# The first layer of a graph network: the product of the two e columns moved from VectorE to TensorE, shift and clamp in one operation

## The chip, the cores and the metric

The kernel runs on one core of a Trainium2 chip. A core has a matrix engine (TensorE, PE in the profile), a vector engine (VectorE, DVE), an engine for activation functions (ScalarE, ACT), a general engine (GpSimd, POOL) and SyncE (SP), which here only issues DMAs. Each engine takes its instructions in program order; they meet through semaphores. Matmuls write to PSUM[...]; everything else lies in SBUF or in DRAM. The metric is the device time of one launch in microseconds, and less is better.

## The reference, cut to what matters

Four graph layers follow each other on 4096 nodes with 128 features, each added to its input and normalised. Only the first, a hyperbolic graph convolution, is touched. With h the nodes as points of the unit ball it computes

```python
x_tangent = logmap0(h)
x_local = jax.vmap(lambda xi: logmap(xi, h))(h)          # 4096 x 4096 x 128, never formed by the kernel
logits = (x_tangent @ wl)[:, None] + (x_tangent @ wr)[None, :] + att_b[0]
adj_att = adj * jax.nn.sigmoid(logits)
support_t = jnp.einsum('ij,ijd->id', adj_att, x_local)
```

logmap(xi, hj) is a multiple of the Moebius difference of the two points, so the sum over j needs, for each pair (i, j), one scalar factor that depends on the distance alone, and products with matrices of node features. The kernel scales the nodes to g, takes e = sqrt(1/4 + g.g) for each node, and finds the factor from

t(i, j) = e(i) e(j) - g(i).g(j), not less than 1/4 + 5e-7,

as log(4t + 2s) / s, where s is the square root of 4t*t - 1/4. The factor is symmetric in i and j, the sigmoid is not.

## The kernel before

The rows and columns of the 4096 x 4096 matrices are cut into eight blocks of 512. `pair_loop` goes over the 36 pairs of blocks (I, J) with I not above J; each of the 28 pairs of two different blocks serves both (I, J) and (J, I), the 8 diagonal ones serve one side. Each tile of a pair has 128 partitions and 4 x 512 elements. For one pair the steps of the work are:

- `load`: the 512 x 512 adjacency block of each side comes from DRAM by SP (1 MB each; two buffers). On a new row of pairs it also broadcasts the rows di and ei to all partitions, otherwise dj.
- `turn_adj`, four (or eight) times: PE transposes 512 x 128 of it into PSUM (ptA, two buffers). `copy` takes the result to the tile `at` on ScalarE, `vcopy` does the same on VectorE. `store` writes `at` to DRAM for the later layers.
- `distance`, four times: PE multiplies g by g into PSUM (pz, two buffers, which it shares with `turn`).
- `shift`, four times: VectorE forms t from the broadcast row ei, the column ex and pz, in one scalar_tensor_tensor: ei * ex - pz.
- `clamp`: VectorE takes the maximum of the whole tile and the lower limit into y.
- `square`, `ln`, `root`, `inverse`, `log` on ScalarE, `add_root` and `phi` on VectorE: the factor, in the tile t.
- `sigmoid` on ScalarE (four activations a side), `mask` on VectorE (times the adjacency), `first` on VectorE (times the factor).
- `turn` on PE (the factor transposed, four times) and `second` on VectorE (times it), for the other side of the pair.
- `sum_i`, `sum_j` on PE: the products with the features; `add_i`, `add_j` on VectorE: added up.

The order is written out by hand in `PAIR_ORDER` (line 32 on): a list of entries name.k.ahead. In step i each entry is issued for pair i + ahead, so work of up to five pairs stands side by side; the list sets the order in every engine's queue, and nothing reorders it later. Adjacency blocks with k of 4 or more, `turn`, `second`, `sum_j` and `add_j` are left out for a diagonal pair. ScalarE works with sets of tables: sigmoid is in one set, logarithm and exponential in another, and a change between them is an instruction of its own. `sigmoid` loads the second set after its last side (line 609).

Ahead of the loop `layer0` computes the columns. e lies in the second half of the tile `de` (line 395, ex at line 411) beside d, the column of the logits; PE turns `de`, ScalarE evacuates it (line 428) and SP stores it as `rows` in DRAM (line 429), from where the broadcasts take it.

Of the kernel before, what the change touches and what calls it, by code (L numbers as in the profile page):

```python
# [9 lines left out]
F32 = mybir.dt.float32  # L10
F32R = mybir.dt.float32r
AF = mybir.ActivationFunctionType
ALU = mybir.AluOpType
# [3 lines left out]
P = 128  # L17
# [7 lines left out]
S = 512  # L25
# [4 lines left out]


PAIR_ORDER = """
turn_adj.4.0 first.0.-1 copy.4.0 distance.2.1 second.3.-1 mask.0.0 ln.0.0 turn_adj.1.1 turn.1.-1
root.0.0 sum_i.1.-2 turn_adj.0.1 shift.2.1 copy.1.1 copy.0.1 mask.1.0 load.1.1 add_i.0.-2 add_root.0.0
store.1.0 sum_j.0.-2 distance.1.1 turn_adj.3.1 turn_adj.5.1 inverse.0.0 sum_i.0.-1 second.1.-1
add_j.0.-2 distance.0.1 log.0.0 shift.1.1 sigmoid.0.1 vcopy.3.1 distance.3.1 turn_adj.2.1 add_j.1.-2
vcopy.5.1 sum_i.3.-1 phi.0.0 shift.0.1 load.0.2 turn_adj.7.1 sum_i.2.-1 copy.2.1 turn.2.0 shift.3.1
clamp.0.1 turn.0.0 turn_adj.6.1 vcopy.7.1 sigmoid.1.1 second.2.0 copy.6.1 second.0.0 square.0.1
sum_j.1.-1 store.0.1 turn.3.0
"""  # L40


class Net:
# [226 lines left out]
    def layer0(self, x, weight, bias, att_w, att_b):  # L270
        nc, tc, N, NT, D = self.nc, self.tc, self.N, self.NT, self.D
# [3 lines left out]
        with ExitStack() as ctx:  # L275
# [4 lines left out]
            pre = pre_pools.enter_context(tc.tile_pool(name="pre0", bufs=2))  # L280
# [4 lines left out]
            HT = keep.tile([P, N], F32, tag="HT", name="HT")  # L285
            HA = keep.tile([P, NT, D + 1], F32, tag="HA", name="HA")
# [31 lines left out]
            p = self.ps_t.tile([P, 4, P], F32, tag="pt", name="pt")  # L318
# [14 lines left out]
            for g in self.groups():  # L333
                s = slice(g[0], g[-1] + 1)
                p = self.ps_t.tile([P, 4, P], F32, tag="pt", name="pt")
# [55 lines left out]
            b = self.ts("b", hsq, -1.0, ALU.mult, 1.0, ALU.add)  # L391
            nc.vector.tensor_scalar(b, b, MIN_NORM, None, op0=ALU.max)
            rb = self.rec("rb", b)
            ga, gb = self.tt("ga", ca, rb, ALU.mult), self.tt("gb", cb, rb, ALU.mult)
            de = self.cols.tile([P, 2, NT], F32, tag="de", name="de")
            gg = self.col("gg")
            for g in self.groups():
                p = self.ps_t.tile([P, 4, P], F32, tag="pt", name="pt")
# [9 lines left out]
                nc.gpsimd.tensor_tensor(squares[:, 0, :, :], H[:, s, :], H[:, s, :], ALU.mult)  # L408
                nc.vector.tensor_reduce(gg[:, s], squares[:, 0, :, :], AX.X, ALU.add)

            ex = de[:, 1, :]
            nc.vector.tensor_scalar(ex, gg, 0.25, None, op0=ALU.add)
            nc.scalar.activation(ex, ex, AF.Sqrt)
            nc.vector.tensor_scalar(rb, ex, 0.5, None, op0=ALU.add)
            nc.vector.reciprocal(b, rb)

            at = self.artanh_over("ah", hn)
            dl, dr = de[:, 0, :], self.col("dr")
# [2 lines left out]
                nc.vector.scalar_tensor_tensor(d, cb, hw[:, k : k + 1], d, op0=ALU.mult, op1=ALU.add)  # L421
                nc.vector.tensor_tensor(d, d, at, ALU.mult)
            nc.vector.tensor_scalar(dl, dl, attb, None, op0=ALU.add)
            rows = self.dram.tile([2, N], F32, tag="rows", name="rows")
            p = self.ps_t.tile([P, 4, P], F32, tag="pt", name="pt")
            nc.tensor.transpose(p[0 : 2 * NT, 0, :], de.rearrange("p k t -> p (k t)"), self.ident)
            e2 = pre.tile([2 * NT, P], F32, tag="e2", name="e2")
            nc.scalar.copy(e2, p[0 : 2 * NT, 0, :])
            nc.sync.dma_start(out=rows.rearrange("k (t p) -> (k t) p", p=P), in_=e2)
            b2x, bhalf = self.ts("b2x", b, 2.0, ALU.mult), self.ts("bhalf", b, 0.5, ALU.mult)  # L430

            hp1 = self.ts("hp1", b, -1.0, ALU.mult, 2.0, ALU.add)
# [2 lines left out]
            nc.vector.memset(self.quarter, -0.25)  # L435

            pre_pools.close()
            self.pair_loop(HT, HA, dr, ex, rows)


            x0 = HT.rearrange("p (t d) -> p t d", d=D)
# [70 lines left out]
                if t % 4 == 3:  # L512
                    self.normalise_tile(t // 4, on_scalar=True)

    def pair_loop(self, HT, HA, dr, ex, rows):

# [2 lines left out]
        nc, tc, NS, D = self.nc, self.tc, self.NS, self.D  # L521
        with ExitStack() as ctx:
# [3 lines left out]
            wk = ctx.enter_context(tc.tile_pool(name="wk0", bufs=2))  # L526
# [4 lines left out]
            pairs = [(I, J) for I in range(NS) for J in range(I, NS)]  # L531
            n = len(pairs)
            st = [{} for _ in pairs]
            row = {}

            def sides(p):

                I, J = pairs[p]
                return [(I, J)] if I == J else [(I, J), (J, I)]

            def broadcast(k, I, tag):

                t = wk.tile([P, S], F32, tag=tag, name=tag)
                nc.sync.dma_start(out=t, in_=rows[k, I * S : (I + 1) * S].partition_broadcast(P))
                return t

            def once(p, key, pool, tag, shape=(4, S), **kw):

                if key not in st[p]:
                    st[p][key] = pool.tile([P, *shape], F32, tag=tag, name=tag, **kw)  # L550
                return st[p][key]

            def load(p, k):
                I, J = pairs[p]
                if k == 0:
                    if I == J:
                        row["d", I] = broadcast(0, I, "di")
                        row["e", I] = broadcast(1, I, "ei")
                    else:
                        row["d", J] = broadcast(0, J, "dj")  # L560
                    st[p]["d"] = [row["d", i] for i, _ in sides(p)]
                    st[p]["e"] = row["e", I]
                i, j = sides(p)[k]
                nc.sync.dma_start(
                    out=once(p, f"ad{k}", adp, "ad"),
                    in_=self.adj[i * S : (i + 1) * S, j * S : (j + 1) * S].rearrange("(a p) c -> p a c", p=P),
                )

            def turn_adj(p, m):
                pt = ps_t.tile([P, 4, P], F32, tag="pt", name="ptA")  # L570
# [14 lines left out]
            def distance(p, b):  # L585
                I, J = pairs[p]
                pz = ps_z.tile([P, S], F32, tag="pz", name="pz")
                j = 4 * J + b
                nc.tensor.matmul(  # L589
                    pz, lhsT=HT[:, j * P : (j + 1) * P], rhs=HT[:, I * S : (I + 1) * S], start=True, stop=True  # L590
                )
                st[p]["pz", b] = pz

            def shift(p, b):
                j = 4 * pairs[p][1] + b
                nc.vector.scalar_tensor_tensor(  # L596
                    once(p, "t", wk, "t")[:, b, :], st[p]["e"], ex[:, j : j + 1], st[p].pop(("pz", b)),
                    op0=ALU.mult, op1=ALU.subtract,
                )

            def sigmoid(p, k):
                J = sides(p)[k][1]
                w = once(p, f"w{k}", wtp, "w")
                for jb in range(4):
                    nc.scalar.activation(  # L605
                        w[:, jb, :], st[p]["d"][k], AF.Sigmoid, bias=dr[:, 4 * J + jb : 4 * J + jb + 1]
                    )
                if k == len(sides(p)) - 1:
                    nc.scalar.preload_act_table_set("natural_log_exp_and_others")

            def mask(p, k):
                w = st[p][f"w{k}"]
                nc.vector.tensor_tensor(w, w, st[p][f"at{k}"], ALU.mult)  # L613

            def clamp(p, _):
                y = once(p, "y", wk, "y", bufs=1)
                nc.vector.tensor_scalar(y, st[p]["t"], 0.25 + 5e-7, None, op0=ALU.max)

            def square(p, _):
                nc.scalar.activation(st[p]["y"], st[p]["y"], AF.Square, scale=2.0)  # L620

            def ln(p, _):
                nc.scalar.activation(st[p]["y"], st[p]["y"], AF.Ln, bias=self.quarter)

            def root(p, _):
                nc.scalar.activation(once(p, "s", wk, "s", bufs=1), st[p]["y"], AF.Exp, scale=0.5)

            def inverse(p, _):
                nc.scalar.activation(st[p]["y"], st[p]["y"], AF.Exp, scale=-0.5)

            def add_root(p, _):
# [1 line left out]
                nc.vector.scalar_tensor_tensor(t, t, 2.0, st[p]["s"], op0=ALU.mult, op1=ALU.add)  # L633

            def log(p, _):
                t = st[p]["t"]
                nc.scalar.activation(t, t, AF.Ln, scale=2.0)

# [63 lines left out]
            def add_i(p, _):  # L702
# [7 lines left out]
            whole = {"load", "store", "sigmoid", "mask"}  # L710
            work = dict(
                load=load, turn_adj=turn_adj, copy=copy, vcopy=vcopy, store=store, distance=distance, shift=shift,
                sigmoid=sigmoid, mask=mask, clamp=clamp, square=square, ln=ln, root=root, inverse=inverse,
                add_root=add_root, log=log, phi=phi, first=first, turn=turn, second=second, sum_i=sum_i, sum_j=sum_j,
                add_j=add_j, add_i=add_i,
            )
            order = [(name, int(k), int(ahead)) for name, k, ahead in (o.split(".") for o in PAIR_ORDER.split())]

            def step(i):


                for name, k, ahead in order:
                    p = i + ahead
                    if not 0 <= p < n:
                        continue
                    two = len(sides(p)) == 2
                    if two or not (
                        name in pair_only or name in whole and k == 1 or name in blocks and k >= 4
                    ):
                        work[name](p, k)  # L730

            reach = [ahead for _, _, ahead in order]
# [814 lines left out]
```

## Time and profile before

| what | us |
|---|---|
| median of 3 runs (2209.81 to 2211.59) | 2210.46 |
| the profiled execution, of which the times below come | 2210.88 |
| its span, from the first to the last instruction | 2209.1 |
| ahead of the pair loop, 0 to 71 | 71 |
| the pair loop, 71 to 774 | 703 |
| the rest: the end of the first layer and the three other layers | 1435 |

In the stretch from 71 to 774 us TensorE is busy for 579.4 us, VectorE for 672.7, ScalarE for 678.9 and GpSimd for 26.7 (the last of it work for what follows the loop). The DMA engines have a mean share of 0.62.

The groups of the loop that the change touches, from the page of the whole execution:

| line and operation | count | mean ns |
|---|---|---|
| L596 VectorE, shift, 512 elements, one operand in PSUM | 144 | 740 |
| L617 VectorE, clamp, 2048 elements | 36 | 1231 |
| L577 ScalarE, adjacency copy from PSUM, 512 elements | 164 | 578 |
| L577 VectorE, the same copy | 92 | 683 |
| L589 PE, records of the distances (two to a matmul) | 288 | 628 |

How to read the views: a line of the page gives the source line, the engine, the operation, output and inputs with their sizes, the count, the busy time with the mean of one, and the idle time just before with what ended it. A line of the timeline gives start, length, engine, line, operation, tiles and the number of neighbours merged; in brackets stands how long the engine was idle before and what released it. A row of the windows view gives a stretch, its length, and how long each engine was busy in it with its number of instructions, then the clock of TensorE that was granted, the share of the DMA engines' time and what they moved.

### The profile page before, as it was taken

The numbers are of one execution on the slowest core, as the hardware profiler recorded it, in microseconds if no ns is written. First come the engines' busy times: TensorE is split into PE (matmuls) and PEld (weight loads), VectorE is DVE, ScalarE is ACT, GpSimd is POOL, SyncE is SP. The second block draws the span as 40 slices with busy tenths as digits, with TensorE's granted clock in tenths as the row PEclk, the third lists the DMA queues.
The fourth block names the chain that finished last, engine by engine and source line by source line (L and its number), as shares of the span: only waits on it lengthen the run. The fifth ranks groups of instructions, "written<-read, shape, count | busy, mean of one in ns | idle before, by whom it ended". The sixth has DMA issues, their size and how long they took to land.

```text
span 2209.1 us, 24056 instructions
## 1 busy us (share of the span) xinstructions
PE 1947.3 (88%) x8720; PEld 1048.7 (47%) x8720; DVE 1882.1 (85%) x2732; ACT 1476.3 (67%) x1858; POOL 105.7 (5%) x146
## 2 busy tenths in 40 slices
PE   4488888888888708999999999999998999989998
PEld 4266666666666605433333333333333444434443
DVE  6699999999999987789999999999897344558887
ACT  5699999999999974687777787877883222210000
POOL 2000000000000432210000000000000000000000
PEclk7689999999999956999999999999998999999999
DMA  2466566666666407884646465565456777767883
GB/s 55 143 210 234 205 243 209 229 200 228 213 208 212 156 0 246 210 229 172 198 163 190 172 198 181 174 191 175 169 194 232 281 269 272 254 234 270 290 300 111
DMA packets 112868, 448.44 MB, mean 203 GB/s; under 512 B 9760, under 2 KB 20064, under 8 KB 71776
## 3 DMA queue, kind: packets, MB, share of 16 engines
q1 hardware_dynamic: 94160, 361.82, 46.5%
q10 hardware_dynamic: 9360, 68.16, 9.1%
q0 software_dynamic: 9216, 16.78, 4.2%
q8 instruction: 73, 1.20, 0.2%
q14 instruction: 59, 0.48, 0.1%
HBM read 369.10 MB, written 77.63 MB: 202 GB/s over the span
## 4 chain that ended last, share of the span: by engine, by line
PE 41%; DVE 34%; ACT 17%; issue 5%; DMA 3%; ACTq 0%; POOL 0%; SPq 0%; DVEq 0%; POOLq 0%
PE pv L919 10%; PE pa L1253 10%; PE pa L1430 9%; DVE e L902 8%; PE ps L893 5%; DVE w L613 3%; ACT e L900 3%; ACT w L605 3%; DVE t L596 2%; DVE w L645 2%; DVE nat L883 2%; DVE t L641 2%; DVE w L656 2%; DVE t L633 1%; ACT at L577 1%
## 5 line engine op out<-in xcount | busy, mean ns | idle before, releaser
L902 DVE SCALAR_TENSOR_TENSOR e<-at,e 128x2048 f32<-128x2048 f32 x256 | 583.0, 2287 | 70.2 <-ACT e L900 69.5
L900 ACT ACTIVATE e<-ps 128x1024 f32<-128x1024 f32 x512 | 493.3, 1024 | 146.9 <-PE ps L893 126.1
L919 PE MATMUL pv<-e,VA 128*64 128x512 f32 x2048 | 497.0, 606 | 7.1 <-DVE e L902 6.3
L893 PE MATMUL ps<-QS,KS 128*128 128x512 f32 x1024 | 313.0, 425 | 4.3 <-issue 2.0
L893 PEld LDWEIGHTS ps<-QS,KS 128*128 128x128 f32 x1024 | 172.0, 189 | 230.0 <-ACT e L900 173.4
L919 PEld LDWEIGHTS pv<-e,VA 128*64 128x64 f32 x2048 | 124.9, 136 | 249.3 <-issue 214.8
L1253 PE MATMUL pa<-ring,Y 128*128 128x512 f32 x512 | 229.2, 602 | 0.0
L573 PE MATMUL ptA<-ident,ad 128*128 128x128 f32 x1024 | 158.5, 283 | 62.0 <-ACT at L577 50.0
L1430 PE MATMUL pa<-w,F 128*128 128x512 f32 x448 | 197.0, 598 | 0.0
L573 PEld LDWEIGHTS ptA<-ident,ad 128*128 128x128 f32 x1024 | 119.8, 144 | 142.0 <-ACT at L577 98.0
L1427 DVE SCALAR_TENSOR_TENSOR w<-rho,col,ring 128x512 f32<-128x512 f32 x224 | 162.8, 747 | 25.5 <-PE pa L1430 13.1
L589 PE MATMUL pz<-HT 128*128 128x512 f32 x288 | 151.3, 628 | 22.1 <-DVE w L656 16.5
L668 PE MATMUL pi<-HA,w 128*128 128x129 f32 x1152 | 154.4, 279 | 0.8 <-DVE w L645 0.8
L1253 PEld LDWEIGHTS pa<-ring,Y 128*128 128x128 f32 x512 | 97.4, 194 | 114.3 <-issue 113.8
L613 DVE TENSOR_TENSOR w<-w,at 128x2048 f32<-128x2048 f32 x64 | 146.1, 2283 | 0.5 <-ACT at L577 0.5
L668 PEld LDWEIGHTS pi<-HA,w 128*128 128x128 f32 x1152 | 142.2, 195 | 4.0 <-issue 2.3
L1430 PEld LDWEIGHTS pa<-w,F 128*128 128x128 f32 x448 | 84.3, 191 | 107.2 <-issue 79.5
L874 ACT ACTIVATE nat<-nat 128x2048 f32<-128x2048 f32 x64 | 122.6, 1916 | 3.5 <-DMA nat<-in_adj_dram 3.5
L596 DVE SCALAR_TENSOR_TENSOR t<-ei,de,pz 128x512 f32<-128x512 f32 x144 | 103.8, 740 | 16.0 <-PE pz L589 8.4
L683 PE MATMUL pj<-HA,w 128*128 128x129 f32 x896 | 109.5, 274 | 2.7 <-DVE w L656 2.7
L683 PEld LDWEIGHTS pj<-HA,w 128*128 128x128 f32 x896 | 104.6, 191 | 2.9 <-DVE w L656 2.9
L577 ACT COPY at<-ptA 128x512 f32<-128x512 f32 x164 | 91.2, 578 | 14.2 <-PE ptA L573 13.8
(359 smaller groups left out, 2443.8 us busy)
## 6 DMA issues: line engine op xcount, KB each, us to landing
ring<-adjT SPq DMA_DIRECT2D x128, 1024.0 KB, 5.1
ad<-in_adj_dram SPq DMA_DIRECT2D x64, 1024.0 KB, 5.3
adjT<-at SPq DMA_DIRECT2D x64, 1024.0 KB, 4.9
nat<-in_adj_dram ACTq DMA_DIRECT2D x64, 1024.0 KB, 5.0
at<-adjT SPq DMA_DIRECT2D x63, 1024.0 KB, 4.8
qk<-cut SPq DMA_DIRECT2D x16, 512.0 KB, 11.4
KS<-qk POOLq DMA_DIRECT2D x32, 256.0 KB, 7.6
QS<-qk POOLq DMA_DIRECT2D x32, 256.0 KB, 5.3
```

Source lines behind the costliest of these rows:

```text
L573: nc.tensor.transpose(pt[:, ib, :], ad[:, ib, jb * P : (jb + 1) * P], self.ident)
L589: nc.tensor.matmul(pz, lhsT=HT[:, j * P : (j + 1) * P], rhs=HT[:, I * S : (I + 1) * S], start=True, stop=True)
L613: nc.vector.tensor_tensor(w, w, st[p][f"at{k}"], ALU.mult)
L668: nc.tensor.matmul(row[I, "po"][ib // 2][:, ib % 2, :], lhsT=st[p]["w0"][:, jb, ib * P : (ib + 1) * P], rhs=HA[:, 4 * J + jb, :], start=False,
L683: nc.tensor.matmul(pj[:, a, :], lhsT=st[p]["w1"][:, ib, jb * P : (jb + 1) * P], rhs=HA[:, 4 * I + ib, :], start=(ib == 0), stop=(ib == 3),)
L893: nc.tensor.matmul(p[:, h, :], lhsT=KS[:, h2 + h, jb * P : (jb + 1) * P], rhs=QS[I % 2][:, h2 + h, :], start=True, stop=True,)
L900: nc.scalar.activation(e[:, h2 : h2 + 2, :], p, AF.Exp)
L902: nc.vector.scalar_tensor_tensor(e, at[:, jb % 4, :].unsqueeze(1).to_broadcast([P, NH, S]), 0.0, e, op0=ALU.not_equal, op1=ALU.mult,)
L919: nc.tensor.matmul(st["po"][h // 2][g : g + 64, :], lhsT=VA[:, o : o + 64], rhs=e[:, h, :], start=(jb == 0), stop=(jb == NT - 1), skip_gro ...
L1253: nc.tensor.matmul(st["pa"], lhsT=Y[:, 4 * J + jb, :], rhs=at[:, jb, :], start=False, stop=(J == NS - 1 and jb == 3), skip_group_check=True,)
L1427: nc.vector.scalar_tensor_tensor(w, rho[:, I * S : (I + 1) * S], col[:, 0, j : j + 1], at[:, jb, :], op0=ALU.max, op1=ALU.mult)
L1430: nc.tensor.matmul(pa, lhsT=F[:, j, :], rhs=w, start=False, stop=(j == NT - 1), skip_group_check=True)
```

## The change

The product e(i) e(j) is computed by PE and added to the distances in the PSUM tile, so that pz holds g.g - e.e. Each e is split into two parts, which the type float32r (one pass of PE) holds: the first rounded, the second what is left, rounded. The four products of parts are four contraction rows of one matmul: `er` holds the rows (part 1, part 2, part 1, part 2) for block I, `el` the negated rows (1, 1, 2, 2) for block J. `shift` is then one tensor_scalar from PSUM: times -1, maximum with the lower limit. `clamp` and ei are gone; `square` reads t and writes y.

What else changes: `layer0` makes the parts on VectorE, turns three columns instead of two, evacuates the turned tile twice (plain on ScalarE, negated on VectorE) and stores five rows with two DMAs. A function `vectors`, called at the head of every step for the pair farthest ahead, issues the di and dj broadcasts on SP and the loads of er and el on GpSimd (which converts to float32r). The change of tables is now placed in front of the first logarithm or exponential after a sigmoid. And `PAIR_ORDER` is another list: among other things the loads come later, `first` and `mask` of a pair's second side stand a step behind, four adjacency blocks of eight go to VectorE (0, 1, 2, 6) instead of three (3, 5, 7).

```diff
-turn_adj.4.0 first.0.-1 copy.4.0 distance.2.1 second.3.-1 mask.0.0 ln.0.0 turn_adj.1.1 turn.1.-1
-root.0.0 sum_i.1.-2 turn_adj.0.1 shift.2.1 copy.1.1 copy.0.1 mask.1.0 load.1.1 add_i.0.-2 add_root.0.0
-store.1.0 sum_j.0.-2 distance.1.1 turn_adj.3.1 turn_adj.5.1 inverse.0.0 sum_i.0.-1 second.1.-1
-add_j.0.-2 distance.0.1 log.0.0 shift.1.1 sigmoid.0.1 vcopy.3.1 distance.3.1 turn_adj.2.1 add_j.1.-2
-vcopy.5.1 sum_i.3.-1 phi.0.0 shift.0.1 load.0.2 turn_adj.7.1 sum_i.2.-1 copy.2.1 turn.2.0 shift.3.1
-clamp.0.1 turn.0.0 turn_adj.6.1 vcopy.7.1 sigmoid.1.1 second.2.0 copy.6.1 second.0.0 square.0.1
-sum_j.1.-1 store.0.1 turn.3.0
+turn_adj.2.0 mask.1.-1 second.0.-1 turn.1.-1 copy.3.0 turn.2.-1 vcopy.2.0 square.0.0 second.1.-1 ln.0.0
+turn_adj.1.0 turn.3.-1 second.2.-1 vcopy.1.0 first.0.-1 distance.3.1 load.1.0 turn_adj.6.0 sum_j.0.-2
+turn_adj.4.0 second.3.-1 add_j.1.-2 root.0.0 copy.4.0 sum_i.0.-1 distance.2.1 shift.3.1 vcopy.6.0
+load.0.1 turn_adj.5.0 add_root.0.0 distance.1.1 inverse.0.0 copy.5.0 log.0.0 turn_adj.7.0 shift.2.1
+mask.0.0 sum_i.3.-1 distance.0.1 store.0.0 phi.0.0 turn_adj.0.1 copy.7.0 shift.1.1 shift.0.1 store.1.0
+sigmoid.1.0 sum_i.1.-1 sum_i.2.-1 sigmoid.0.2 turn_adj.3.1 vcopy.0.1 add_j.0.-2 add_i.0.-1 turn.0.0
+sum_j.1.-1
...
-            de = self.cols.tile([P, 2, NT], F32, tag="de", name="de")
+            de = self.cols.tile([P, 3, NT], F32, tag="de", name="de")
...
-            ex = de[:, 1, :]
+            ex = self.col("ex")
...
+            for k in range(2):
+                part = self.cols.tile([P, NT], F32R, tag="part", name="part")
+                nc.vector.tensor_copy(part, ex)
+                nc.vector.tensor_copy(de[:, 1 + k, :], part.bitcast(F32))
+                if k == 0:
+                    nc.vector.tensor_tensor(ex, ex, de[:, 1, :], ALU.subtract)
...
-            nc.tensor.transpose(p[0 : 2 * NT, 0, :], de.rearrange("p k t -> p (k t)"), self.ident)
-            e2 = pre.tile([2 * NT, P], F32, tag="e2", name="e2")
-            nc.scalar.copy(e2, p[0 : 2 * NT, 0, :])
-            nc.sync.dma_start(out=rows.rearrange("k (t p) -> (k t) p", p=P), in_=e2)
+            nc.tensor.transpose(p[0 : 3 * NT, 0, :], de.rearrange("p k t -> p (k t)"), self.ident)
+            e2 = pre.tile([P, 2, P], F32, tag="e2", name="e2")
+            nc.scalar.copy(e2[0 : 3 * NT, 0, :], p[0 : 3 * NT, 0, :])
+            nc.vector.tensor_scalar(e2[0 : 3 * NT, 1, :], p[0 : 3 * NT, 0, :], -1.0, None, op0=ALU.mult)
+            nc.sync.dma_start(out=rows[0:3, :].rearrange("k (t p) -> (k t) p", p=P), in_=e2[0 : 3 * NT, 0, :])
+            nc.sync.dma_start(out=rows[3:5, :].rearrange("k (t p) -> (k t) p", p=P), in_=e2[NT : 3 * NT, 1, :])
...
-                t = wk.tile([P, S], F32, tag=tag, name=tag)
+                t = wk.tile([P, S], F32, tag=tag, name=tag, bufs=2 if tag == 'di' else 4)
...
+            def vectors(p):
+                I, J = pairs[p]
+                if I == J:
+                    row["d", I] = broadcast(0, I, "di")
+                    er = row["er", I] = wk.tile([4, S], F32R, tag="er", name="er", bufs=2)
+                    for k in range(2):
+                        nc.gpsimd.dma_start(out=er[2 * k : 2 * k + 2, :], in_=rows[1:3, I * S : (I + 1) * S])
+                else:
+                    row["d", J] = broadcast(0, J, "dj")
+                st[p]["d"] = [row["d", i] for i, _ in sides(p)]
+                el = st[p]["el"] = wk.tile([4, S], F32R, tag="el", name="el", bufs=3)
+                for k in range(2):
+                    nc.gpsimd.dma_start(
+                        out=el[2 * k : 2 * k + 2, :], in_=rows[3 + k, J * S : (J + 1) * S].partition_broadcast(2)
+                    )
...
-                    pz, lhsT=HT[:, j * P : (j + 1) * P], rhs=HT[:, I * S : (I + 1) * S], start=True, stop=True
+                    pz, lhsT=HT[:, j * P : (j + 1) * P], rhs=HT[:, I * S : (I + 1) * S], start=True, stop=False
+                )
+                nc.tensor.matmul(
+                    pz, lhsT=st[p]["el"][:, b * P : (b + 1) * P], rhs=row["er", I], start=False, stop=True
                 )
...
-                nc.vector.scalar_tensor_tensor(
-                    once(p, "t", wk, "t")[:, b, :], st[p]["e"], ex[:, j : j + 1], st[p].pop(("pz", b)),
-                    op0=ALU.mult, op1=ALU.subtract,
+                nc.vector.tensor_scalar(
+                    once(p, "t", wk, "t")[:, b, :], st[p].pop(("pz", b)), -1.0, 0.25 + 5e-7, op0=ALU.mult, op1=ALU.max
                 )
...
-                if k == len(sides(p)) - 1:
+                tables.add("sigmoid")
+
+            def logs_and_exps():
+                if tables:
                     nc.scalar.preload_act_table_set("natural_log_exp_and_others")
+                    tables.clear()
...
-            def clamp(p, _):
-                y = once(p, "y", wk, "y", bufs=1)
-                nc.vector.tensor_scalar(y, st[p]["t"], 0.25 + 5e-7, None, op0=ALU.max)
-
             def square(p, _):
-                nc.scalar.activation(st[p]["y"], st[p]["y"], AF.Square, scale=2.0)
+                nc.scalar.activation(once(p, "y", wk, "y", bufs=1), st[p]["t"], AF.Square, scale=2.0)
...
+                if 0 <= i + max(reach) < n:
+                    vectors(i + max(reach))
```

`ln`, `root`, `inverse` and `log` call `logs_and_exps` first.

## The prediction

> **What bounds the kernel now.** I read the page first (parts 1 and 2, to find the first layer's stage), then the windows view for three neighbouring steps of its pair loop, then the timeline of VectorE and ScalarE in one step, and last the timeline of the start. The pair loop runs from about 71 to 774 us. A step is one pair of 512-row blocks (28 of two different blocks, 8 on the diagonal).
>
> ```profile
> core 0: us, PE busy (x) PEld busy (x) DVE busy (x) ACT busy (x) POOL busy (x), PEclk, DMA share, GB/s
> 161.84:181.59 19.75, 17.15 (x122) 13.65 (x121) 19.72 (x20) 19.66 (x21) 0.00 (x0) 1.00 0.64 227
> 181.59:201.34 19.75, 17.16 (x122) 13.65 (x122) 19.72 (x20) 19.43 (x21) 0.00 (x0) 1.00 0.63 227
> 221.10:240.17 19.07, 15.90 (x113) 12.73 (x113) 19.04 (x18) 18.75 (x21) 0.00 (x0) 1.00 0.66 235
> 240.17:257.13 16.96, 15.45 (x110) 12.56 (x109) 16.93 (x19) 16.73 (x15) 0.00 (x0) 1.00 0.41 139
> 257.13:275.72 18.59, 15.65 (x108) 12.36 (x107) 18.16 (x19) 18.50 (x21) 0.00 (x0) 1.00 0.68 241
> ```
>
> The first two rows are full steps: 19.75 us, VectorE 19.72 and ScalarE 19.43 to 19.66 of it. Both are full; unloading only one would bring almost nothing. The last three rows lie around a diagonal pair. DMA at 0.64 is not the limit, and GpSimd does nothing here.
>
> ```profile
> 201.26 2.28 DVE L641 TENSOR_TENSOR t<-t,y 128x2048 f32<-128x2048 f32 x1
> 203.46 1.40 DVE L596 SCALAR_TENSOR_TENSOR t<-ei,de,pz 128x512 f32<-128x512 f32 x2
> 204.90 1.23 DVE L617 TENSOR_SCALAR y<-t 128x2048 f32<-128x2048 f32 x1
> 206.04 0.68 DVE L577 COPY at<-ptA 128x512 f32<-128x512 f32 x1
> 206.64 1.28 DVE L656 TENSOR_TENSOR w<-w,ptz 128x512 f32<-128x512 f32 x2
> ...
> 214.91 1.05 ACT L577 COPY at<-ptA 128x512 f32<-128x512 f32 x2
> 215.85 1.93 ACT L629 ACTIVATE y<-y 128x2048 f32<-128x2048 f32 x1
> 218.01 1.91 ACT L637 ACTIVATE t<-t 128x2048 f32<-128x2048 f32 x1 [0.23 <-DVE t L633]
> ```
>
> Start-to-start, not duration, is what an instruction costs an engine, since neighbours overlap. VectorE from 201.26 to the next start of the same line at 221.02: L641, L645, L633 and two L613 at 2.20 each, shifts (L596) 0.66 to 0.78, clamp (L617) 1.14, copies 0.60, L656 0.60, additions 0.33. They sum to 19.76 without a gap. ScalarE from 198.26 to 218.01: 19.52 of work and the 0.23 wait shown; a copy costs 0.47.
>
> **What the Trainium skill says.** "VectorE: DVE Perf Modes", Why PSUM operands drop a tier: an fp32 operation with a PSUM operand runs one element a cycle, while tensor_scalar within SBUF runs two. The trace agrees: the clamp takes 1231 ns for 2048 elements, the copy from PSUM 683 ns for 512. "TensorE: Matmul & The Clock Gate", Back-to-back issue gap: N/2.4 + 2.5 ns, so 216 ns for 512 columns. The two fp32r matmuls of the second layer in one row (0.63 us for two, 397 ns median for one) fit with 0.23; a full fp32 distance is two records 0.43 apart, so 0.86. "SBUF — State Buffer", Who interferes with whom: VectorE with two SBUF inputs contends with GpSimd's reads and not with its writes. The new row loads are issued from GpSimd beside such instructions; in the second layer GpSimd issues four DMAs in 2.15 us beside L902, which never takes more than 2294 ns (median 2286), so I charge VectorE nothing.
>
> **The change part by part.**
>
> *VectorE.* The clamp goes: 1.14 and the longer handover before it (0.78 against 0.66), so 1.26. The shift becomes a tensor_scalar with two constants from PSUM, which this trace does not show. The nearest rows are the copy from PSUM (683 ns) and rho<-psr at L1328 (751, with a column as operand); the present shift is 740, also with a column. I take the copy: 0.06 less each, 0.24 a step; at worst nothing. The order gives VectorE four adjacency copies instead of three: +0.60. So 19.76 - 1.26 - 0.24 + 0.60 = 18.86, or 19.10 at worst.
>
> *ScalarE.* One of five copies goes: 19.52 - 0.47 = 19.05. Square reads t directly and writes y; table loads stay two a step, since the flag only moves the second one behind the square.
>
> *Diagonal pairs.* ScalarE drops from three copies to one, VectorE rises from one to three. Over the loop ScalarE loses 28 + 2 x 8 = 44 copies at 0.47, 20.7 us. VectorE loses 36 x 1.26 = 45.4, and 144 x 0.06 = 8.6 or nothing, and gains 44 x 0.60 = 26.4: 27.6 or 19.0 less. Both ends lie near 20, so whichever is full, about 20 goes. I take ScalarE's 20.7, with its idle time (5.0 us of the 595.9 between 161.84 and 757.73) as it is.
>
> *TensorE.* Its start-to-starts in a step: transposes 12 x 0.44, sums 8 x 0.90, distances 4 x 0.87, together 16.0. The product adds four fp32r matmuls at 0.22: 16.9. At 19.05 that leaves 2.1 us for waits on others. I laid the new order out by these durations: turn.2 waits 1.2 us for second.0, three others 0.1 to 0.3 each, and every result is ready before its reader, the closest being second.2 (0.4 us) and log after add_root (0.3 us). It fits with little to spare. I charge 3 us over the loop, with 0 to 10 as ends.
>
> *Loads.* Per step SP holds dj, load.1.0, load.0.1, store.0.0, store.1.0. Load.1.0 stands behind store.1.0 of the step before, which waits for copy.7; it issues some 4 us before the step begins, and its first reader comes 6 us into it: 10 us for a transfer of 5.3. Load.0.1 is freed by turn_adj.1, is issued 4 us in, is read at 14.5. The ei broadcasts (8 x 256 KB) go from SP. The 88 small row loads on GpSimd at 0.54 (the KS and QS issues) are 48 us on an engine that is idle; a row load is issued a whole step before its reader, against 17.1 for the slowest landing among the second layer's DMAs on qk, which hold the trace's only GpSimd loads, and after the first two pairs GpSimd runs ahead until it meets the three-buffer ring.
>
> *Start.* It runs in the open:
>
> ```profile
> 70.68 0.54 SPq L429 DMA_DIRECT2D rows<-e  x1
> 72.57 0.34 SPq L544 DMA_DIRECT2D di<-rows  x1
> 73.49 0.38 SPq L564 DMA_DIRECT2D ad<-in_adj_dram  x1
> 81.51 1.94 PE L573 MATMUL ptA<-ident,ad 128*128 128x128 f32 x8 [8.73 <-DMA ad<-in_adj_dram]
> 82.69 0.59 ACT L577 COPY at<-ptA 128x512 f32<-128x512 f32 x1 [12.03 <-PE ptA L573]
> ```
>
> Between the square root and the transpose five small operations are inserted on VectorE (with those between, about 1.7 us at 0.1 to 0.35 each), then a second evacuation (0.3) and a second store in front of di (0.5): rows land 2.5 us later, and the adjacency with them. Four distances now run ahead of the first transposes on a cold TensorE (PEclk 0.50 from 70 to 81.5), some 2 us more. Against that, eight sigmoids and a table load (6.4 us) run while ScalarE waits for the adjacency (12 us idle). Net -2, between -6 and +4.
>
> **The sum.** -20.7 - 2 + 3 = -20 against the profiled execution's own 2210.9 us (span 2209.1, 1.8 around it): 2190.9. The median of the runs is 0.4 lower: 2190.5.
>
> **The rivals.**
>
> *The gain is partly eaten by queue order, 0.17.* TensorE is in order and has 2.1 us free a step instead of 3.75. Between 110 and 700 us its weight loads for the adjacency transposes already wait 78 us, in 66 pieces, for ScalarE's copies. If each step loses 0.3 more than laid out, 36 x 0.3 = 10.8 comes back: 2201. For it: two PSUM buffers for every kind of tile. Against it: the step now runs at 19.75 with the same buffers and no engine but TensorE waiting.
>
> *Nothing is gained, 0.08.* The same at 0.6 a step, or add_root and phi fall out of step with ScalarE (the 0.23 wait shown, doubled twice): 36 x 0.55 = 20 gives 2210.
>
> *TensorE becomes the bound, slower, 0.13.* The place is the distance and its product. The step is 16.0 + four products + 1.3 of unavoidable waits; from 0.61 us for a product on, it is over 19.76. If the fp32r product of four rows, inside an accumulation that an fp32 matmul opens, costs a full distance (0.86), the step is 20.7: 36 x 1.0, less 2 at the start, gives 2244. For it: no matmul of this shape or mixture is in the trace. Against it: L893 and the price that the skill's TensorE page states.
>
> *The forecast, 0.62,* holds 2182 to 2199: VectorE's worst shift (+2), TensorE's waits (-3 to +7), the start (-4 to +6).
>
> **The numbers.** A measurement of this kernel can tell 0.2% (4.4 us) from no change. Forecast and partly eaten gain are faster: 0.79. Same 0.08, slower 0.13. The range 2180 to 2207 takes in the forecast, the eaten gain and half of the no-gain case; about 0.17 lies above it and 0.03 below.
>
> **What would show it.** In full steps of the new trace: a distance from one phi to the next of 19.0 to 19.2; shifts at 0.68 us; no L617 of 2048 elements; 120 copies on ScalarE and 136 on VectorE (164 and 92 before); the product's matmul 0.22 after the distance's second record; TensorE busy near 18 a step; first sigmoids before the first adjacency copy. It is wrong if steps last 19.5 or more, with VectorE or ScalarE waiting for TensorE (the gain eaten or TensorE the bound), if the product takes over 0.6, or if TensorE waits for the row loads.

## The result: no change that can be measured, 19 us short of the forecast

| | us |
|---|---|
| before, median of 4 runs (2209.81 to 2211.59) | 2210.56 |
| changed, median of 4 runs (2206.33 to 2213.44) | 2209.18 |
| ratio, with its 95% interval | 0.9995 (0.9978 to 1.0012) |
| forecast, with its range | 2190.5 (2180 to 2207) |
| profiled execution, before and changed | 2210.88 and 2208.76 |
| its span, before and changed | 2209.1 and 2207.0 |

First the steps, since the forecast rests on them. The windows view of the changed kernel, from one phi (now L665) to the next, for two full steps (columns as in the same view before):

```profile
core 0: us, PE busy (x) PEld busy (x) DVE busy (x) ACT busy (x) POOL busy (x), PEclk, DMA share, GB/s
162.46:181.50 19.04, 18.54 (x125) 13.99 (x124) 18.94 (x21) 18.71 (x20) 2.06 (x4) 1.00 0.73 236
181.50:200.66 19.16, 18.88 (x126) 14.24 (x126) 19.04 (x20) 19.05 (x20) 1.03 (x2) 1.00 0.72 235
```

A full step takes 19.04 to 19.16 us instead of 19.75, as forecast. VectorE and ScalarE are still full, but TensorE now is too: 18.5 to 18.9 of it, against 17.15 of 19.75. So the gain was there, and the question is where it went. Cut at the first and the last phi, the execution has three parts. The windows view of the middle part, first of the kernel before, then of the changed one:

```profile
100.84:762.20 661.36, 554.12 (x3733) 432.42 (x3732) 649.97 (x621) 653.99 (x658) 14.88 (x12) 0.99 0.63 217
```

```profile
105.32:752.79 647.47, 616.85 (x3873) 451.92 (x3873) 627.32 (x619) 632.83 (x612) 48.33 (x83) 0.98 0.68 218
```

| part | before | changed | difference |
|---|---|---|---|
| to the first phi | 100.8 | 105.3 | +4.5 |
| first to last phi | 661.4 | 647.5 | -13.9 |
| last phi to the end | 1446.9 | 1454.2 | +7.3 |
| span | 2209.1 | 2207.0 | -2.1 |

In the middle part ScalarE works 21.2 us less (653.99 to 632.83), near the 20.7 forecast for 44 copies; its idle time, the difference to the stretch, grew from 7.4 to 14.6 us. A start that should have gained 2 us lost 4.5. And the last part, which the change does not touch, is 7.3 us longer. Each of the three was followed.

**The middle.** The view of ScalarE's waits in that stretch, before and then changed (total us, times, longest):

```profile
ACT t L637 <- DVE t L633: 2.0, 8, 0.4
ACT at L577 <- PE ptA L573: 1.5, 1, 1.5
```

```profile
ACT at L596 <- PE ptA L592: 6.9, 13, 3.4
ACT t L661 <- DVE t L656: 3.5, 7, 1.0
```

ScalarE's copies now wait for the turned adjacency, 6.9 us against 1.5; the other 1.5 of growth in the list are waits for VectorE. The timeline of TensorE, changed kernel, shows that its queue is longer than forecast:

```profile
209.91 1.13 PE L608 MATMUL pz<-HT 128*128 128x512 f32 x2
210.97 0.49 PE L611 MATMUL pz<-er,el 4*128 4x512 f32 x1
211.39 0.66 PE L592 MATMUL ptA<-ident,ad 128*128 128x128 f32 x4
```

From the product's start to the next start it is 0.42 us, not 0.22; and the second record of the distance before it takes 0.52 us to the next start where it took 0.43 with transposes behind it. So a product takes some 0.51 us of TensorE.

Half of the 6.9 us is one wait, and it stands at a stretch of low clock. TensorE's clock is at 0.50 from 103.2 to 120.3 us in this profile. In the profile of e1 (below), which has the same loop, it is at 0.50 from 102.5 to 112.7 only, and the same copy does not wait, first changed, then e1:

```profile
121.76 0.59 ACT L596 COPY at<-ptA 128x512 f32<-128x512 f32 x1 [3.41 <-PE ptA L592]
```

```profile
117.92 0.59 ACT L596 COPY at<-ptA 128x512 f32<-128x512 f32 x1
```

e1's middle part takes 644.3 us, 3.2 less, with 3.4 us of waits for ptA.

**The start.** The timeline of TensorE and ScalarE, changed kernel:

```profile
81.75 0.76 PE L611 MATMUL pz<-er,el 4*128 4x512 f32 x1 [7.51 <-DMA el<-rows]
82.44 2.08 PE L608 MATMUL pz<-HT 128*128 128x512 f32 x2
84.44 0.79 PE L611 MATMUL pz<-er,el 4*128 4x512 f32 x1
...
90.62 2.59 PE L592 MATMUL ptA<-ident,ad 128*128 128x128 f32 x10
...
77.25 5.00 ACT L625 ACTIVATE w<-di,dr 128x512 f32<-128x512 f32 x8 [4.16 <-DMA di<-rows]
92.62 0.58 ACT L596 COPY at<-ptA 128x512 f32<-128x512 f32 x1 [10.37 <-PE ptA L592]
```

The sigmoids do run in ScalarE's idle time (77.25). But the first product waits until 81.75 for the row loads, with the other three distances and the adjacency's transposes behind it in TensorE's queue. A distance and its product then take 2.7 us each (82.44 to 85.17, the next distance) at a granted clock of 0.50, so the transposes begin at 90.62 (before: 81.51, shown in the prediction).

**The end.** The third layer, in `layers23`, reads the adjacency again from a ring of 1 MB blocks that SP loads. Its first VectorE instruction on the ring is `odd`, which counts values other than 0 and 1. The timeline of VectorE there, before and then changed:

```profile
1697.86 2.29 DVE L1261 SCALAR_TENSOR_TENSOR odd<-ring 128x2048 f32<-128x2048 f32 x1 [3.77 <-DMA br<-in_L_gnn_b_dram]
```

```profile
1694.74 2.29 DVE L1287 SCALAR_TENSOR_TENSOR odd<-ring 128x2048 f32<-128x2048 f32 x1 [9.95 <-DMA ring<-adjT]
```

The wait grew by 6.2 us, and the rest of VectorE's queue stands behind it. The releaser named, a ring load, can't be it: TensorE had used the ring's first block from 1678.22 on. The changed kernel's waiting instructions of this line, in two short windows, show VectorE's queue going on in two pieces:

```profile
L1287 DVEq EVENT_SEMAPHORE  x4: 21/50/50, 1689.3 to 1689.6; - x4
```

```profile
L1287 DVEq EVENT_SEMAPHORE  x5: 21/50/50, 1694.3 to 1694.8; - x5
```

And the DMA view of the 13 us up to that instruction has in it, among queues of kind "instruction", two fetches on q14 before and six in the changed kernel:

```profile
q14 instruction: 2, 0.02, 0.3%
```

```profile
q1 hardware_dynamic: 792, 4.79, 94.6%
q14 instruction: 6, 0.05, 0.9%
```

Instructions themselves come by DMA, through engines that the data transfers of q1, the ring loads among them, fill to 94.6%. That gave a theory: the change adds 44 entries to VectorE's program ahead of this place, and the end of a fetched piece fell between the waits of the first odd. The rivals were late data and chance.

### The profile page after: what moved, and what is told of

Read it like the earlier page. It is cut to its first block, busy times and chain, and to the rows that moved or that the text cites. A ratio compares the mean times of both kernels' runs of the same rounds, so it can differ in the third digit from the quotient of the medians.

```text
span 2207.0 us, 24491 instructions
## 1 busy us (share of the span) xinstructions
PE 2011.9 (91%) x8864; PEld 1064.7 (48%) x8864; DVE 1859.6 (84%) x2746; ACT 1455.6 (66%) x1814; POOL 149.8 (7%) x234
## 3 DMA queue, kind: packets, MB, share of 16 engines
q0 software_dynamic: 12032, 17.15, 4.3%
## 4 chain that ended last, share of the span: by engine, by line
PE 45%; DVE 29%; ACT 18%; issue 5%; DMA 3%; SPq 0%; POOL 0%; ACTq 0%; DVEq 0%; POOLq 0%
PE pa L1279 10%; PE pv L945 9%; DVE e L928 9%; PE pa L1456 9%; PE ps L919 5%; ACT e L926 4%; ACT w L625 3%; DVE w L637 3%; DVE nat L909 2%; DVE t L656 2%; PE pz L608 2%; ACT y L644 2%; PE pa L1302 1%; ACT y L640 1%; DMA ad<-in_adj_dram 1%
## 5 line engine op out<-in xcount | busy, mean ns | idle before, releaser
L608 PE MATMUL pz<-HT 128*128 128x512 f32 x288 | 160.2, 639 | 4.2 <-DVE t L617 3.5
L1279 PEld LDWEIGHTS pa<-ring,Y 128*128 128x128 f32 x512 | 97.0, 193 | 113.4 <-issue 112.7
L617 DVE TENSOR_SCALAR t<-pz 128x512 f32<-128x512 f32 x144 | 95.7, 686 | 21.0 <-PE pz L611 20.9
L656 DVE SCALAR_TENSOR_TENSOR t<-t,s 128x2048 f32<-128x2048 f32 x36 | 82.5, 2291 | 15.8 <-ACT s L648 15.1
```

The lines of the kernel that those rows point to most:

```text
L608: nc.tensor.matmul(pz, lhsT=HT[:, j * P : (j + 1) * P], rhs=HT[:, I * S : (I + 1) * S], start=True, stop=False)
L1279: nc.tensor.matmul(st["pa"], lhsT=Y[:, 4 * J + jb, :], rhs=at[:, jb, :], start=False, stop=(J == NS - 1 and jb == 3), skip_group_check=True,)
```

## The experiments

Times are medians; a ratio is to the kernel before, run beside it on the same chip. The first phi and the parts are those of the one profiled execution of each kernel.

**e1 and e2: only the place of VectorE's instructions.** Counted in the built program, the first odd is VectorE's 5980th entry before (92 past a multiple of 128) and the 6024th in the changed kernel (8 past one). `attention_shifted`, a branch ahead of that place, does not run here; memsets put into it shift what follows and are never executed. To the changed kernel (60) and to the kernel before (44):

```diff
             self.on_scalar = 0
+            for _ in range(60):
+                nc.vector.memset(bt, 0.0)
```

> The changed kernel with 60 VectorE memsets in attention_shifted, the branch that does not run: nothing that runs is changed, only the place of VectorE's later instructions in its program (the first odd of the third layer's opening moves from 8 past a multiple of 128 to 68 past one). Theory A, the opening's lost 6 to 7 us are a fetch of VectorE's own instructions that queues behind the ring loads: the 9.95 us wait ahead of the first odd falls to about 4, odd starts about 10 us after the first product of pa instead of 16.5, and the time is about 2203 us (2209.2 less 6). Theory B, the opening waits for the ring's data or differs from run to run by chance: the wait stays near 10 us, or moves without a pattern, and the time is 2209.

> The kernel before with 44 VectorE memsets in the branch that does not run, which puts VectorE's first odd at the same place of its program as in the changed kernel (8 past a multiple of 128). Theory A (instruction fetch): the wait ahead of the first odd grows from 3.77 to about 10 us, and the time from 2210.5 to about 2216.5. Theory B: wait 3.8, time 2210.5, as before.

Measured: e1 2206.31 us, 0.9983 (0.9976 to 0.9989) of the kernel before; e2 2217.15 us, 1.0029 (1.0018 to 1.0040). The same line of VectorE's timeline in e1, then in e2:

```profile
1688.45 2.29 DVE L1289 SCALAR_TENSOR_TENSOR odd<-ring 128x2048 f32<-128x2048 f32 x1 [4.83 <-DMA ring<-adjT]
```

```profile
1704.55 2.29 DVE L1263 SCALAR_TENSOR_TENSOR odd<-ring 128x2048 f32<-128x2048 f32 x1 [9.45 <-DMA ring<-adjT]
```

The wait follows the place in both directions: the kernel before becomes 7 us slower by instructions that never run. All twelve profiles agree: 8.95 to 9.95 us in the seven kernels with the odd at 7 or 8 past a multiple of 128 (five or six fetches on q14 in the 13 us), 4.83 to 5.60 in the three at 68 (three fetches), 3.77 and 4.54 in the two at 92 (two fetches). The part from the last phi to the end falls into the same three groups: 1452.0 to 1459.1 us, 1448.0 to 1451.0, and 1446.4 to 1446.9. Theory A holds. Its size for the whole time was forecast too high for e1: in the profiles 3.7 of the 7.3 us came back. The median fell by 2.9 us, which alone would be within the interval of the changed kernel's four runs. Of the 3.6 us left, 1.1 are the wait itself (4.83 against 3.77); the other 2.5 were not traced.

**e3: the product left out.**

```diff
-                    pz, lhsT=HT[:, j * P : (j + 1) * P], rhs=HT[:, I * S : (I + 1) * S], start=True, stop=False
-                )
-                nc.tensor.matmul(
-                    pz, lhsT=st[p]["el"][:, b * P : (b + 1) * P], rhs=row["er", I], start=False, stop=True
+                    pz, lhsT=HT[:, j * P : (j + 1) * P], rhs=HT[:, I * S : (I + 1) * S], start=True, stop=True
```

> The changed kernel without the product matmul (the e times e part of every distance is left out; the loads of its rows stay). Theory P, the product crowds TensorE so that the turned adjacency comes late to ScalarE: ScalarE's wait for ptA within the loop (6.9 us) falls below 3, the loop from the first phi to the last goes from 647.5 to about 642, and TensorE's busy time there falls by 144 times 0.42, some 60 us. Theory O, the new order alone makes ScalarE wait: loop 647 still. In both the first distances no longer wait for the rows, so that the first phi comes some 8 us earlier. Time: P 2196, O 2201.

Measured: 2193.52 us, 0.9923 (0.9908 to 0.9939). The windows view from first to last phi:

```profile
97.52:736.50 638.98, 552.57 (x3732) 441.59 (x3731) 626.19 (x618) 630.91 (x612) 39.60 (x67) 0.97 0.68 221
```

TensorE works 64.3 us less (616.85 to 552.57), 0.47 for each of the 137 products in the stretch. The wait for ptA is gone from ScalarE's list, whose only entry is:

```profile
ACT t L658 <- DVE t L653: 4.2, 7, 1.8
```

The stretch is 8.5 us shorter, and 5.0 shorter than the shortest profile with the product in this order (e8's 643.98). So theory P: it is the product, not the new order alone, that makes ScalarE wait. Late adjacency is not the cause: an adjacency load lands 8.2 us after its issue in the changed kernel (5.3 before, which the prediction had taken), but it takes 8.0 here too, and TensorE waits for loads a little longer here (5.4 us) than with the product (3.7). And the first phi is at 97.52: without the product the new order's start is 3.3 us earlier than the old one's, with it 4.5 later. The product's start costs 7.8.

**e4: the product twice.**

```diff
+                nc.tensor.matmul(
+                    pz, lhsT=st[p]["el"][:, b * P : (b + 1) * P], rhs=row["er", I], start=False, stop=False
+                )
                 nc.tensor.matmul(
                     pz, lhsT=st[p]["el"][:, b * P : (b + 1) * P], rhs=row["er", I], start=False, stop=True
```

> The changed kernel with the product matmul issued twice (e times e is counted twice). Theory P, a product costs TensorE 0.42 us and TensorE is nearly full: 18.6 us of a 19.1 us step become 20.3, full steps of about 20.5 us, the loop some 40 us longer, 2250 us. The price of the prediction, 0.22 us for each: 19.5 of a step, loop some 12 us longer, 2221 us.

Measured: 2224.02 us, 1.0060 (1.0045 to 1.0076); from first to last phi 659.34, 11.9 longer, with ScalarE's wait for ptA at 19.3 us. That is the second expectation, and TensorE's timeline shows that neither had the whole of it:

```profile
230.56 1.13 PE L608 MATMUL pz<-HT 128*128 128x512 f32 x2
231.61 0.50 PE L611 MATMUL pz<-er,el 4*128 4x512 f32 x1
231.95 0.39 PE L614 MATMUL pz<-er,el 4*128 4x512 f32 x1
232.28 0.66 PE L592 MATMUL ptA<-ident,ad 128*128 128x128 f32 x4
```

Two products take 0.67 us where one takes 0.42. A second product adds 0.25, near the forecast's 0.22; with the 0.09 by which the distance is longer, some 0.26 more are paid once, where the float32 distance and the float32r product meet.

**e6: product first, then the distance.** The two matmuls exchanged, with start and stop.

> The changed kernel with the two matmuls of a distance exchanged: product first (it opens the PSUM tile), then the 128-row distance. The second of two products in a row cost about 0.16 to 0.2 us where the first costs 0.43. Theory T1, the extra 0.2 us is paid at each change from a float32 matmul to a float32r one, in whichever order: TensorE's busy time in the loop stays near 615 us, ScalarE's wait for ptA at 3 to 7, loop 644 to 648. Theory T2, it is the product's weights that cannot be loaded while the float32 distance runs: with the product first its weights load behind transposes, which frees about 0.2 times 144 = 29 us of TensorE, ScalarE's wait for ptA falls below 2, loop about 642. The start is later or the same in both: the first distance itself now waits for the rows at a low clock (first phi 105 to 107).

Measured: 2211.84 us, 1.0004 (0.9995 to 1.0012); TensorE busy 619.26 in the stretch of 649.19, the first phi at 107.66. Nothing is freed, as T1 has it; that the extra is a cost of changing the type, and not of the first product of four rows, was not tried apart. The part after the last phi was 3 to 7 us longer than in the other profiles of its group; this was not followed.

**e5, e7 and e8: the start.** e5 keeps TensorE busy while it waits for the rows; e7 halves the row transfers; e8 is both with the 60 memsets of e1.

```diff
+                if p == 0 and b == 3:
+                    for _ in range(6):
+                        nc.tensor.matmul(
+                            pz, lhsT=HT[:, j * P : (j + 1) * P], rhs=HT[:, I * S : (I + 1) * S], start=True, stop=True
+                        )
```

```diff
-                    for k in range(2):
-                        nc.gpsimd.dma_start(out=er[2 * k : 2 * k + 2, :], in_=rows[1:3, I * S : (I + 1) * S])
+                    nc.gpsimd.dma_start(
+                        out=er, in_=rows[1:3, I * S : (I + 1) * S].unsqueeze(0).to_broadcast([2, 2, S])
+                    )
...
-                for k in range(2):
-                    nc.gpsimd.dma_start(
-                        out=el[2 * k : 2 * k + 2, :], in_=rows[3 + k, J * S : (J + 1) * S].partition_broadcast(2)
-                    )
+                nc.gpsimd.dma_start(
+                    out=el, in_=rows[3:5, J * S : (J + 1) * S].unsqueeze(1).to_broadcast([2, 2, S])
+                )
```

> The changed kernel with six more issues of the first pair's first distance matmul ahead of the real one (into the same PSUM tile, overwritten by it), so that TensorE works from 72 to about 81.7 us instead of waiting for the row loads with its clock falling. Theory S1, half of the lost start is the low clock: products still begin near 81.75, but the four distances take 1.5 us each instead of 2.7, adjacency transposes begin at 86 to 87 instead of 90.6, the first phi comes at about 100 instead of 105.3, the time falls by 4 to 5 us against the changed kernel (2209) to 2204 or 2205. Theory S2, only the rows' arrival counts, because the adjacency's copies or ScalarE set the first phi: first phi 104 to 105, time 2208 to 2209.

> The changed kernel with er and el each loaded by one transfer instead of two (the same rows, repeated by the transfer's pattern). GpSimd then issues er and the first pair's el in about 1.2 us instead of 2.3. If the start waits for the issue of these loads, the first product comes about 1.1 us earlier (80.6), the first phi at about 104.2, the time 1 us less (2208); if landing sets it, whatever the number of transfers, nothing moves.

> The changed kernel with three of these edits together: 60 memsets in the branch that does not run, the six extra matmuls ahead of the first distance, and er and el in one transfer each. If the gains add up: first phi near 99 instead of 105.3, the opening's wait 4 to 5 us instead of 10: 2209 less 3 (median with the moved instructions) less 5 to 6, 2200 to 2201 us. If the start's gain is not kept to the end of the loop (a later wait takes it): 2206.

Measured: e5 2205.56 us, 0.9979 (0.9970 to 0.9987); e7 2207.03 us, 0.9984 (0.9977 to 0.9990); e8 2196.56 us, 0.9937 (0.9923 to 0.9951). In the profiles e5's first phi is at 104.81, not near the 100 of S1, and e7's at 106.07, with the first product at 82.50 (nothing moved); in e8 it is at 99.92. TensorE's timeline tells why, first e5, then e8:

```profile
79.25 1.02 PE L613 MATMUL pz<-HT 128*128 128x512 f32 x2
81.93 0.47 PE L616 MATMUL pz<-er,el 4*128 4x512 f32 x1 [1.65 <-DMA el<-rows]
82.33 1.68 PE L613 MATMUL pz<-HT 128*128 128x512 f32 x2
83.94 0.79 PE L616 MATMUL pz<-er,el 4*128 4x512 f32 x1
84.66 2.08 PE L613 MATMUL pz<-HT 128*128 128x512 f32 x2
```

```profile
80.27 1.02 PE L613 MATMUL pz<-HT 128*128 128x512 f32 x2
81.22 0.50 PE L616 MATMUL pz<-er,el 4*128 4x512 f32 x1
81.65 1.12 PE L613 MATMUL pz<-HT 128*128 128x512 f32 x2
82.71 0.50 PE L616 MATMUL pz<-er,el 4*128 4x512 f32 x1
83.13 1.12 PE L613 MATMUL pz<-HT 128*128 128x512 f32 x2
...
86.10 1.09 PE L592 MATMUL ptA<-ident,ad 128*128 128x128 f32 x8
```

The extra matmuls do bring TensorE to full speed (1.02 us for a distance at 79.25). In e5 they end 1.65 us before the rows land, and within a distance of that gap it is at half speed again (2.08). In e8 there is no gap, a distance with its product takes 1.48 us, and the transposes begin at 86.10. So S1 was right that much of the loss is the clock: with it up, 5.4 of the product's 7.8 us came back. In e5's profiled execution filling most of the wait did not do. That execution (2208.89) is slower than e5's median, and its 19 runs go from 2197.93 to 2210.76; whether the clock stayed up in the fast ones is not known.

**e9: the second gap.** e8 leaves a wait of 5 us ahead of the second pair's last distance, in which the clock falls again (0.50 from 95 to 105 us). Nine more matmuls into pi, then unused, fill it.

> The three edits together, and nine matmuls into a PSUM tile that is not yet in use (pi, which its opening overwrites) where TensorE waits some 5 us for VectorE ahead of the second pair's last distance, and after which its clock was low for 10 us in the three edits together and for 17 us in the changed kernel. If this second stretch at a low clock makes ScalarE wait in some executions (3.4 to 4.6 us ahead of one copy in four of the profiles, nothing in two), the clock stays at 1.00 from 80 us on, no wait for ptA is over 0.6 us, the spread of the times gets smaller and the median falls from 2196.6 to 2194 or 2195. If the spread comes from elsewhere: 2196 to 2197, as wide as before.

Measured: 2198.34 us, 0.9947 (0.9933 to 0.9960). The clock stayed at 1.00 to 100 us but was at 0.50 for 3.4 us from 103.8 and for 6.8 from 124.3; ScalarE's wait for ptA was 6.4 us in this profile, 3.3 in e8's. It gave nothing.

*The spread.* The times of one kernel spread widely (the changed kernel from 2206 to 2213, e1 from 2201 to 2211 in 21 runs). For the loop the profiles show where it comes from. In the seven that have the new order and one product (changed, e1, e5 to e9) the first-to-last-phi stretch runs from 644.0 to 651.3 us and ScalarE's wait for ptA from 3.3 to 10.9; the stretch less this wait is 640.4 to 641.2 in all of them. Eleven of these waits are over 1 us, and each begins in a piece of low clock or within 2 us of its end. Without the product such pieces cost nothing: e3 has seven in its stretch and no wait for ptA. So the product takes the slack with which TensorE had made up for a low clock. That the runs without a profile spread for the same reason is not shown.

**e10: the warm start for the kernel before.** Eight extra issues of its first distance.

> The kernel before with eight more issues of its first distance matmul ahead of the real one, so that its TensorE works through the wait for the adjacency too. If the warm start is worth to the kernel before what it is worth to the changed one, the first phi comes 3 to 5 us earlier (96 to 98 instead of 100.8) and the time falls to 2206 to 2207, and of the 14 us of the three edits together only 9 to 10 are the change's. If the kernel before doesn't wait for TensorE's clock (its adjacency is turned at 81.5 and copied one block at a time): first phi 100, time 2209 to 2210, and all 14 us are out of reach for it.

Measured: 2208.59 us, 0.9990 (0.9983 to 0.9997), first phi at 100.10. The kernel before gains 2.3 us by it, so some 12 of e8's 14 us (2210.51 to 2196.56) are out of its reach by this means. e8 beats both kernels.

## Why the prediction was wrong

Three terms of the sum failed: the start, the price of the product on TensorE, and the rest of the execution, which the sum put at nothing. In us of the profiled executions:

| term | forecast | measured | shown by |
|---|---|---|---|
| ScalarE's 44 copies | -20.7 | -21.2 of work | the windows |
| waits that TensorE causes in the loop | +3 (0 to 10) | +5.4 for ptA; +7.3 of ScalarE's idle time in all | waits, e3 |
| start | -2 (-6 to +4) | +4.5 | timeline, e3, e8 |
| behind the loop | not in the sum | +7.3 | e1, e2 |
| sum | -20 | -2.1 | |

- *VectorE and ScalarE.* Right. The shift takes 686 ns (683 taken), full steps 19.04 to 19.16 (19.0 to 19.2), and 120 adjacency copies stand on ScalarE.
- *TensorE.* The mechanism was named, the product mis-sized. Its 0.22 was the price of one that follows its like, as in the row it was read from; behind a float32 matmul it is 0.42, and 0.51 with the longer distance. "The Trainium skill", page "TensorE: Matmul & The Clock Gate", Back-to-back issue gap, gives the 216 ns as the gap of a single matmul; this trace comes near it only for the second of two products (0.25). Four products so take 2.0 us of a step instead of 0.9, and of the 2.1 us said to be free about 1 was left. The term itself still came out within its range, and how far is partly luck of the profiled execution: 3.4 of the 5.4 us are the one wait at a low clock, which the prediction did not have at all. In e1's profile the stretch is 17.0 us shorter than before, near the -17.7 of the forecast's first two terms; in e7's it is 10.1. The rival in which TensorE is the bound needed 0.61 a product; it did not come true. e4, whose two products take 0.67, lies above that price, and is 0.6% slower.
- *The start.* This step failed most plainly, by 6.5 us. It charged the rows' stores (the first now issued at 71.82, 1.1 later; 2.5 forecast) and 2 us of cold TensorE, and priced the GpSimd row loads only inside the loop, where they are a step ahead. In the first step nothing is ahead: issued from 73.65 on, the last that the first product needs (at 75.4, landing 6.1 us later) is there near 81.6. The adjacency landed at 80.9 (74.42 and 6.5) and then waits behind four distances at half speed. e3 puts the product's part at 7.8 us: without it the start gains 3.3, near the 2 forecast. "Wrong if TensorE waits for the row loads" was the sign given, and it came.
- *Behind the loop.* The largest error of the three (7.3 us) was not a step at all: the sum assumed that what the diff does not touch keeps its time. Its work and its data were the same; the place of VectorE's instructions was not.
- *The rivals.* "Partly eaten by queue order" had the right place, TensorE's queue, for some of it, but e3 shows the product rather than the order. The result lies in the no-gain case, by none of the mechanisms given for it.

## What to carry to other kernels

Price a matmul by what stands before it in the queue: one short float32r matmul among float32 ones cost 0.51 us, with what it added to the one before; a second in a row added 0.25. When an operand comes by a new load, look at the first step by itself, since there the load is in the open and an in-order engine holds everything behind it; if the wait is filled with work to keep the clock up, look in the trace whether the filling reaches the real work (in e5's profile 1.65 us of gap undid it). When an untouched stage moves by some microseconds after a branch, compare the instruction queues in the DMA view before looking for a cause in the data, and shift the code by instructions that do not run.

## What the runs showed of the hardware

Code that never runs moved the time by 7 us (e2): behind the branch ahead of the third layer, VectorE's instructions are fetched by DMA, about 8 KB each (0.51 MB in 62 fetches), and a second fetch behind four ring loads of 1 MB cost about 5 us (4 waits passed at 1689.3, the next at 1694.3). That q14 is VectorE's queue is read from its counts, which follow VectorE's waits in all twelve profiles.

TensorE's full speed, reached within 7 us of extra matmuls, was lost within about 2 us of a gap of 1.65 us in e5's profile, and kept through 15 us without such a gap (e8, PEclk 0.98 from 80 to 95). Not every such gap costs the clock. At seven places of the loop TensorE waits 1.77 to 1.92 us for VectorE; in the changed kernel's profile the clock fell after three of them and in e1's after one. The first of the three, with the gap from 410.7 us on (slice, length, busy time of each engine, clock, DMA):

```profile
410.43:413.84 3.41, 1.46 (x12) 0.99 (x11) 3.31 (x5) 3.41 (x5) 0.00 (x0) 1.00 0.90 312
413.84:417.26 3.42, 3.42 (x8) 1.48 (x9) 3.42 (x4) 3.39 (x3) 0.00 (x0) 0.50 0.69 195
```

The pieces of low clock in the changed kernel's stretch last 3.4 us or a multiple (17.1, 3.4, 3.4, 6.8). What decides whether a gap brings one was not worked out.
